# A transformer block on one core: one block of time-attention scores a step, layer-norm roots by ScalarE, and other forms of three VectorE operations

## The chip, the core and the metric

The kernel runs on one core of a Trainium2 chip. Five engines work side by side, each through its own instructions in order: TensorE (PE in the profile, its weight loads PEld), VectorE (DVE), ScalarE (ACT), GpSimd (POOL) and SyncE (SP), which here only issues DMA transfers. They wait for one another by semaphores. The metric is the device time of one execution, in microseconds (us). Lower is better.

## The reference, cut to what matters

The input `x` is (B, T, FB, C) = (2, 256, 128, 128) in float32. One layer has three parts, each with a layer norm ahead and a residual sum behind: causal attention along T (4 heads of 32), attention along FB with a band of 16 to each side (4 heads), and a feed-forward with a hidden width of 512.

```python
def _ln(x, w, b, eps=1e-05):
    mu = x.mean(-1, keepdims=True)
    var = ((x - mu) ** 2).mean(-1, keepdims=True)
    return (x - mu) * jax.lax.rsqrt(var + eps) * w + b

def _mha(x, wi, bi, wo, bo, h, mask):
    q, k, v = jnp.split(x @ wi.T + bi, 3, axis=-1)      # ... then split into h heads
    scores = jnp.einsum('...hqd,...hkd->...hqk', q, k) * (1.0 / np.sqrt(dh)) + mask
    attn = jax.nn.softmax(scores, axis=-1)
    o = jnp.einsum('...hqk,...hkd->...hqd', attn, v)
    return o.swapaxes(-2, -3).reshape(x.shape) @ wo.T + bo

xt = _ln(x, ln_t_w, ln_t_b).transpose(0, 2, 1, 3)
x = x + _mha(xt, t_wi, t_bi, t_wo, t_bo, H_T, causal).transpose(0, 2, 1, 3)
xf = _ln(x, ln_f_w, ln_f_b)
x = x + _mha(xf, f_wi, f_bi, f_wo, f_bo, H_F, band)
xn = _ln(x, ln_n_w, ln_n_b)
x = x + (jax.nn.gelu(xn @ w1.T + b1, approximate=False) @ w2.T + b2)
```

## The kernel before

The work is cut into groups of 4 tiles of 128 rows by 128 channels. All 128 `OverTime` groups (two sequences of 256 times in each) come first. Then runs of 8 `OverBands` groups and 8 `FeedForward` groups alternate, 16 runs in all. The software pipeline is a loop over steps `n`, and each step emits one stage of each of several groups: scores of group n, weighing of group n - 1, output of group n - 2, queries, keys and values of group n + 1, and so on down to loads of group n + 11. `InOrder` keeps each engine's instructions in the order in which they are emitted.

The layer norm of a group: statistics by VectorE, root by GpSimd, normalization by VectorE, then a turn to channel-major by a 32x32 transpose and a trip through DRAM.

```python
def root(self):
    self.rstd = path.small.tile([P, NT], F32, name="rstd", bufs=16)
    gpsimd.tensor_scalar(self.rstd, self.mv[:, :, 1], EPS, None, ALU.add)
    gpsimd.tensor_tensor(self.rstd, self.rstd, path.k.mhalf, ALU.pow)

def normalize(self):
    self.xh = path.work.tile([P, NT, P], F32, name="xh", bufs=2)
    for i in range(NT):
        vector.tensor_scalar(
            self.xh[:, i, :], self.src()[:, i, :], self.mv[:, i, 0:1], self.rstd[:, i : i + 1],
            ALU.subtract, ALU.mult,
        )
```

Scores lie as keys by queries. A head has 32 channels, so its scores use 32 rows of TensorE's array, and the four heads stand beside each other in four row tiles (`32*128` in the profile). All other attention products use column tiles (`128*32`) while an attention group is being weighed. In time attention a group has two sequences `s`, each of two key tiles: the first key tile meets 256 queries, the second 128. A step holds the block of `s = 0` at its start and that of `s = 1` after the weighing. Exponentials are by ScalarE, the causal mask by GpSimd, and the denominator takes a sum of two blocks, by GpSimd for `s = 0` and by VectorE for `s = 1`.

```python
class OverTime(Attention):
    W = 3 * P
    def scores(self, s):
        W, a = self.W, 2 * s * P
        self.sp = [path.bank([P, W], "sp") for h in range(H)]
        for h in range(H):
            r = rows_of(h)                                   # 32 rows of the head
            path.tensor.matmul(self.sp[h][:, 0 : 2 * P], self.kT[r, a : a + P], self.qT[r, a : a + 2 * P], ...)
        for h in range(H):
            r = rows_of(h)
            path.tensor.matmul(self.sp[h][:, 2 * P : W], self.kT[r, a + P : a + 2 * P], self.qT[r, a + P : a + 2 * P], ...)
    def weights(self, s):
        for h in range(H):
            path.scalar.activation(self.p[:, s, h, 0 : self.W], self.sp[h], AF.Exp)
    def mask(self, s):
        for n in (2, 0):
            gpsimd.affine_select(out=self.block(s, n), ...)          # 128 x 512
    def add(self, engine, s):
        engine.tensor_tensor(self.block(s, 3), self.block(s, 1), self.block(s, 2), ALU.add)
    # first_half: scores(0); second_half: scores(1); last_sum: add(vector, 1)
    # weigh: op of s = 0, rp (denominators, by a matrix of ones), op of s = 1
```

The division (`rp` and `op` lie in PSUM, the others in SBUF; `r0` is exp(-ln(rp)) by ScalarE, mended by one Newton step) and the band mask:

```python
# Attention.divide
vector.tensor_tensor(by_rows(t), by_tile(self.rp), by_tile(self.r0), ALU.mult)
vector.tensor_tensor(by_rows(u), by_tile(self.op), by_tile(self.r0), ALU.mult)
vector.scalar_tensor_tensor(self.oT, t, 2.0, u, ALU.subtract, ALU.mult)
# OverBands.second_mask, after the exponential; the other three heads are masked by GpSimd
for h in range(H - self.by_vector, H):                       # by_vector = 1
    blk = self.p[:, h]
    vector.tensor_tensor(blk, blk, path.band.unsqueeze(1).to_broadcast([P, NT, P]), ALU.mult)
```

The step, cut to its order:

```python
for n in range(-11, len(groups) + 2):
    do(n + 11, "load")
    do_at(n + 4, OverTime, "statistics")
    do(n, "first_half", "first_function", "first_mask")
    do_at(n + 2, Attention, "fetch")
    do_at(n + 3, Attention, "normalize", "turn")
    do_at(n + 4, OverTime, "root")
    do(n - 1, "weigh", "invert")
    do(n - 1, "divide")
    do(n, "second_half", "second_function", "second_mask", "bias")
    do_at(n + A, OverBands, "bias", "statistics", "root")    # A = 8 groups ahead
    do(n + 1, "queries_keys", "take_query", "take_key")
    do(n - 2, "output", "finish")
    do(n + 1, "values", "take_values")
    do(n, "last_sum")
    # ... cases of FeedForward and of the turns between kinds left out
```

Of the kernel before, what the change touches and what calls it, by code (L numbers as in the profile page):

```python
# [435 lines left out]
class Group:  # L436
# [32 lines left out]

    def normalize(self):  # L470
        path, vector = self.path, self.path.vector
        self.xh = path.work.tile([P, NT, P], F32, name="xh", bufs=2)
        for i in range(NT):
            vector.tensor_scalar(
                self.xh[:, i, :], self.src()[:, i, :], self.mv[:, i, 0:1], self.rstd[:, i : i + 1],
                ALU.subtract, ALU.mult,
            )
# [36 lines left out]
    def last_sum(self):  # L514
        pass

# [31 lines left out]
class Attention(Group):  # L548
    which = None

# [5 lines left out]
    def queries_keys(self):  # L556
        path = self.path
        wf = path.k.wf[self.which]
        self.qp = path.bank([P, NT * P], "qp")
        product(path, self.qp, wf[:, 0:P], self.xnT)  # L560

        self.kp = path.bank([P, NT * P], "kp")
        product(path, self.kp, wf[:, P : 2 * P], self.xnT)
# [11 lines left out]
    def values(self):  # L575
        path = self.path
        wv = path.k.wf[self.which][:, 2 * P : 3 * P]
        self.vp = path.bank([P, NT, P], "vp")
        for i in range(NT):
            product(path, self.vp[:, i], self.xnT[:, i * P : (i + 1) * P], wv)  # L580

    def take_values(self):
        path = self.path
        self.v = path.work.tile([P, NT, P], F32, name="v")
        path.scalar.copy(self.v, self.vp)
# [14 lines left out]
    def divide(self):  # L600

        path, vector = self.path, self.path.vector
        if self.r0 is None:
            self.oT = path.work.tile([P, NT * P], F32, name="oT", bufs=2)
            u = path.work.tile([P, NT * P], F32, name="u", bufs=2)
            vector.tensor_tensor(by_rows(u), by_tile(self.op), by_tile(self.r), ALU.mult)
            vector.tensor_scalar(self.oT, u, -1.0, None, ALU.mult)
            return
        t = path.work.tile([P, NT * P], F32, name="t", bufs=2)
        vector.tensor_tensor(by_rows(t), by_tile(self.rp), by_tile(self.r0), ALU.mult)  # L610
        u = path.work.tile([P, NT * P], F32, name="u", bufs=2)
        vector.tensor_tensor(by_rows(u), by_tile(self.op), by_tile(self.r0), ALU.mult)
        self.oT = path.work.tile([P, NT * P], F32, name="oT", bufs=2)
        vector.scalar_tensor_tensor(self.oT, t, 2.0, u, ALU.subtract, ALU.mult)

    def output(self):
        path = self.path
        self.yp = path.bank([P, NT, P], "yp")
# [22 lines left out]
class OverTime(Attention):  # L641

    which = 0
    W = 3 * P

    def scores(self, s):
        path = self.path  # L650
        W, a = self.W, 2 * s * P
        self.sp = [path.bank([P, W], "sp") for h in range(H)]
        for h in range(H):
            r = rows_of(h)
            path.tensor.matmul(
                self.sp[h][:, 0 : 2 * P], self.kT[r, a : a + P], self.qT[r, a : a + 2 * P], start=True, stop=True
            )
        for h in range(H):
            r = rows_of(h)
            path.tensor.matmul(  # L660
                self.sp[h][:, 2 * P : W], self.kT[r, a + P : a + 2 * P], self.qT[r, a + P : a + 2 * P],
                start=True, stop=True,
            )

    def weights(self, s):
        path = self.path
        for h in range(H):
            path.scalar.activation(self.p[:, s, h, 0 : self.W], self.sp[h], AF.Exp)

    def mask(self, s):  # L670
        path = self.path
        for n in (2, 0):
            blk = self.block(s, n)
            path.gpsimd.affine_select(
                out=blk, in_=blk, compare_op=ALU.is_ge, fill=path.zero, base=0,
                pattern=[[0, H], [1, P]], channel_multiplier=-1,
            )

    def block(self, s, n):
        return self.p[:, s, :, n * P : (n + 1) * P]  # L680

    def add(self, engine, s):
        engine.tensor_tensor(self.block(s, 3), self.block(s, 1), self.block(s, 2), ALU.add)

    def first_half(self):
        self.p = self.path.work.tile([P, 2, H, self.W + P], F32, name="pt", tag="p", bufs=2)
        self.scores(0)

    def first_function(self):
        self.weights(0)  # L690

    def first_mask(self):
        self.mask(0)
        self.add(self.path.gpsimd, 0)

    def second_half(self):
        self.scores(1)

    def second_function(self):
        self.weights(1)  # L700

    def second_mask(self):
        self.mask(1)

    def last_sum(self):
        self.add(self.path.vector, 1)

    def weigh_one(self, op, s):
        path, p, v, W = self.path, self.p, self.v, self.W
        for h in range(H):  # L710
            r = rows_of(h)
            path.tensor.matmul(op[r, s, :], v[:, 2 * s, r], p[:, s, h, 0 : 2 * P], start=True, stop=False)
        for h in range(H):
            r = rows_of(h)
            path.tensor.matmul(
                op[r, s, P : 2 * P], v[:, 2 * s + 1, r], p[:, s, h, 2 * P : W], start=False, stop=True
            )

    def weigh(self):
        path = self.path  # L720
        op = path.bank([P, 2, 2 * P], "op")
        rp = path.bank([P, 2, 2 * P], "rp")
        self.weigh_one(op, 0)
        sums = self.p.rearrange("p s h (n q) -> p s h n q", q=P)[:, :, :, 0:4:3, :]
        for h in range(H):
            path.tensor.matmul(rp[rows_of(h), :, :], path.k.ones[:, 0:D], sums[:, :, h], start=True, stop=True)
        self.weigh_one(op, 1)
        self.op = op.rearrange("p s q -> p (s q)")
        self.rp = rp.rearrange("p s q -> p (s q)")


class OverBands(Attention):
# [14 lines left out]
    def first_function(self):  # L747
        for h in range(H):
            self.path.scalar.activation(self.p[:, h].rearrange("p i q -> p (i q)"), self.sp[h], AF.Exp)
# [11 lines left out]
    def second_mask(self):  # L761
        path = self.path
        for h in range(H - self.by_vector, H):
            blk = self.p[:, h]
            path.vector.tensor_tensor(blk, blk, path.band.unsqueeze(1).to_broadcast([P, NT, P]), ALU.mult)

    def first_half(self):
        self.p = self.path.work.tile([P, H, NT, P], F32, name="pf", tag="p", bufs=2)
        self.scores(range(H))

    def weigh(self):
        path = self.path
        self.rp = path.bank([P, NT * P], "rp")
        for h in range(H):
# [3 lines left out]
            )  # L778
        self.op = path.bank([P, NT * P], "op")
# [7 lines left out]
class FeedForward(Group):  # L787
# [21 lines left out]
    def first_half(self):  # L809
        self.hp = {}  # L810
        self.hT = self.path.work.tile([P, self.path.k.NI, NT * P], F32, name="hT")
# [41 lines left out]
class BoundedPath:  # L853
    def __init__(self, ctx, tc, k):
# [4 lines left out]
        self.ps = ctx.enter_context(tc.tile_pool(name="ps", bufs=8, space=PSUM))  # L859
# [4 lines left out]
        once = ctx.enter_context(tc.tile_pool(name="once", bufs=1))  # L864

        self.band = once.tile([P, P], F32, name="band")
        tc.nc.gpsimd.memset(self.band, 1.0)
        for s in (1, -1):
            tc.nc.gpsimd.affine_select(
                out=self.band, in_=self.band, compare_op=ALU.is_ge, fill=0.0, base=BAND,  # L870
# [3 lines left out]
    def bank(self, shape, name):  # L874
        return self.ps.tile(shape, F32, name=name, tag="ps")
# [12 lines left out]
    def quad(self, held, name, bufs):  # L888

        held[name] = self.xpool.tile([P, NT, NT, P], F32, name=name, tag=name, bufs=bufs)  # L890

    def groups(self, x, out):
# [3 lines left out]
        for b in range(B):  # L896
            for f0 in range(0, FB, GA):
# [17 lines left out]
                def part(name, g, held=held):  # L915
                    if name == "res" and name not in held:
                        self.quad(held, "res", 2)
                    return held[name][:, :, g]
# [3 lines left out]
        for b in range(B):  # L922
            for r0 in range(0, T, RUN):
                run = []
                for t0 in range(r0, r0 + RUN, GB):
# [20 lines left out]
                    def part(name, g, held=held):  # L946
                        if name == "res" and name not in held:
                            self.quad(held, "res", 2)
                        return held[name][:, g]
# [7 lines left out]
    def run(self, x, out):  # L957
# [17 lines left out]
        for n in range(-11, len(groups) + 2):  # L975
            feeds = [at(n - 2 + i, FeedForward) for i in range(5)]
            bands = [at(n - 2 + i, OverBands) for i in range(5)]
            turn = feeds[2] and bands[1]
            self.by_columns = at(n - 1, Attention)
            do(n + 11, "load")  # L980
            do_at(n + 4, OverTime, "statistics")
# [3 lines left out]
            do(n, "first_half", "first_function", "first_mask")  # L985
            if turn:
                do(n, "second_half", "second_function")
            do_at(n + 2, Attention, "fetch")
            do_at(n + 1, FeedForward, "fetch")
            do_at(n + 2, FeedForward, "normalize", "turn")  # L990
            do_at(n + 3, Attention, "normalize", "turn")
            do_at(n + 4, OverTime, "root")
            if bands[2]:
                do(n, "second_mask")
            do(n - 1, "weigh")
            do(n - 1, "invert_exactly" if turn else "invert")
            if bands[2] or turn:
                do(n - 2, "output", "finish")
            do(n - 1, "divide")
            do_at(n + 5, FeedForward, "statistics")  # L1000
            if not turn:
                do(n, "second_half", "second_function")
            if not bands[2]:
                do(n, "second_mask", "bias")
# [3 lines left out]
                if not turn:  # L1008
                    do_at(n + A, OverBands, "statistics", "root")
            do(n + 1, "queries_keys", "take_query", "take_key")  # L1010
            if not bands[2] and not turn:
                do(n - 2, "output", "finish")
            do(n + 1, "values", "take_values")
            do(n, "last_sum")
# [69 lines left out]
```

## Time and profile before

| what | value |
|---|---|
| time, median of 3 runs | 2785.62 us (2785.54 to 2787.24) |
| profiled span | 2785.2 us |
| granted TensorE clock | 0.999 |
| instructions | 103938 |

The profile has one row for each instruction. A float32 product of TensorE stands in it as two matmul instructions. "Busy" is the union of an engine's instructions, and the ends of matmuls are modelled, so that a busy PE does not have to be a PE at its best. Groups are named `out<-in` by the program's tiles: `sp` scores, `pt` and `pf` weights of time and band attention, `op` weighed values, `rp` denominators, `yp` output product, `qp`, `kp`, `vp` query, key and value products, `hp` and `zp` the two feed-forward products, `xh` the normalized rows, `z` and `turned` their turn. Almost all rows carry line L848, that of the helper `InOrder`, so one goes by tiles.

### The profile page before, as it was taken

To read this page: it belongs to the slowest core of one execution; us is meant where nothing else is said; L and a number is where in the kernel's file an instruction comes from. 1 tells how busy PE (TensorE), PEld (TensorE's weight loads), DVE (VectorE), ACT (ScalarE), POOL (GpSimd) and SP (SyncE) were. 2 spreads that over 40 slices of the span, in tenths; PEclk is the share of its full clock that TensorE was granted. 3 is DMA by queue.
4 is the path that set the end of the run, shared out by engine and by line. 5 is a ranking of instruction groups with operands and counts; after the bars stand their busy time and mean duration, and the time that the engine had idled before them with its cause. 6 is when DMAs were issued, how large, how long until landed. Compare 5 with 4: busy or idle time off the path is not lost.

```text
span 2785.2 us, 103938 instructions
## 1 busy us (share of the span) xinstructions
PE 2730.3 (98%) x42534; PEld 1867.5 (67%) x42534; DVE 2221.5 (80%) x6446; ACT 1800.0 (65%) x3328; POOL 2079.3 (75%) x2569
## 2 busy tenths in 40 slices
PE   4999999999999989999999999999999999999998
PEld 3666666666666657776777777777777767767776
DVE  5888888888888898778678687687786786876874
ACT  2888888878888866646556556456466465574563
POOL 3899999999999997667676676676676666766762
PEclk9999999999999999999999999999999999999999
DMA  5555555555555554544544544535545445444333
GB/s 121 135 147 137 137 141 143 146 132 146 139 142 135 146 134 117 129 117 102 140 105 111 132 106 123 130 100 127 127 99 137 104 108 130 113 117 114 91 92 85
DMA packets 471301, 343.70 MB, mean 123 GB/s; under 512 B 43296, under 2 KB 405152, under 8 KB 470816
## 3 DMA queue, kind: packets, MB, share of 16 engines
q1 hardware_dynamic: 469568, 335.92, 47.5%
q8 instruction: 337, 5.52, 0.9%
q14 instruction: 148, 1.21, 0.2%
q10 hardware_dynamic: 1248, 1.05, 0.1%
HBM read 169.03 MB, written 167.77 MB: 121 GB/s over the span
## 4 chain that ended last, share of the span: by engine, by line
PE 93%; DVE 3%; DMA 2%; POOL 1%; issue 0%; SPq 0%; ACT 0%; DVEq 0%; POOLq 0%
PE zp L848 17%; PE hp L848 16%; PE sp L848 12%; PE op L848 10%; PE qp L848 8%; PE rp L848 8%; PE vp L848 8%; PE yp L848 7%; PE kp L848 7%; POOL pt L848 1%; DMA x<-in_x 1%; DVE xh L848 1%; DMA xnT<-turned 1%; DVE oT L848 0%; POOL rstd L848 0%; DVE stats L848 0%
## 5 line engine op out<-in xcount | busy, mean ns | idle before, releaser
L848 ACT ACTIVATE hT<-hp,b 128x512 f32<-128x512 f32 x512 | 348.7, 687 | 546.0 <-PE hp L848 536.1
L848 POOL TENSOR_SCALAR_AFFINE_SELECT pf<-pf 128x512 f32<-128x512 f32 x768 | 541.5, 720 | 173.5 <-ACT pf L848 147.1
L848 PEld LDWEIGHTS zp<-w2T_sb,hT 128*128 128x128 f32 x4096 | 476.4, 192 | 56.1 <-issue 54.0
L848 DVE TENSOR_SCALAR xh<-x,mv,rstd 128x128 f32<-128x128 f32 x1536 | 509.2, 392 | 0.4 <-POOL rstd L848 0.4
L848 PE MATMUL zp<-w2T_sb,hT 128*128 128x128 f32 x4096 | 479.8, 275 | 0.1
L848 PE MATMUL hp<-xnT,w1f 128*128 128x512 f32 x1024 | 469.2, 596 | 3.6 <-DMA xnT<-turned 3.4
L848 POOL TENSOR_TENSOR rstd<-rstd,mhalf 128x4 f32<-128x4 f32 x384 | 441.3, 1149 | 32.0
L848 ACT ACTIVATE pt<-sp 128x384 f32<-128x384 f32 x1024 | 419.5, 497 | 58.8 <-PE sp L848 58.8
L848 PE MATMUL sp<-qT,kT 32*128 32x128 f32 (+1 forms) x8192 | 389.5, 315 | 0.8 <-ACT kT L848 0.8
L848 POOL TENSOR_SCALAR_AFFINE_SELECT pt<-pt 128x512 f32<-128x512 f32 x512 | 322.7, 651 | 79.0 <-ACT pt L848 79.0
L848 PEld LDWEIGHTS sp<-qT,kT 32*128 32x128 f32 x8192 | 310.9, 185 | 79.7 <-issue 31.1
L848 POOL TENSOR_SCALAR rstd<-mv 128x4 f32<-128x4 f32 x384 | 89.2, 232 | 365.5 <-DVE mv L848 365.1
L848 DVE BATCH_NORM_STATS2 stats<-x 128x6 f32<-128x128 f32 x1536 | 329.0, 274 | 7.6 <-DMA x<-in_x 7.6
L848 ACT ACTIVATE pf<-sp 128x512 f32<-128x512 f32 x512 | 264.3, 603 | 58.8 <-PE sp L848 52.4
L848 PEld LDWEIGHTS hp<-xnT,w1f 128*128 128x128 f32 x1024 | 182.2, 190 | 178.9 <-issue 109.6
L848 PE MATMUL qp<-xnT,wf 128*32 128x512 f32 (+1 forms) x1856 | 273.1, 600 | 26.2 <-DVE xh L848 26.2
L848 PEld LDWEIGHTS yp<-wn,oT 128*32 128x32 f32 (+1 forms) x7808 | 240.8, 111 | 84.0 <-issue 63.2
L848 PEld LDWEIGHTS vp<-wf,xnT 128*32 128x32 f32 (+1 forms) x7424 | 241.1, 113 | 70.4 <-issue 60.2
L848 DVE STREAM_TRANSPOSE z<-xh 128x512 f32<-128x512 f32 x384 | 273.2, 711 | 18.9 <-DMA turned<-z 5.8
L848 PE MATMUL yp<-wn,oT 128*32 128x128 f32 (+1 forms) x7808 | 277.9, 273 | 0.3 <-DVE t L848 0.3
L848 DVE TENSOR_TENSOR res<-zp,res 128x512 f32<-128x512 f32 x128 | 87.6, 685 | 234.8 <-PE zp L848 234.7
L848 PE MATMUL vp<-wf,xnT 128*32 128x128 f32 (+1 forms) x7424 | 273.5, 273 | 0.5 <-DVE t L848 0.5
(90 smaller groups left out, 4072.8 us busy)
## 6 DMA issues: line engine op xcount, KB each, us to landing
turned<-z SPq DMA_DIRECT2D x1536, 64.0 KB, 2.2
xnT<-turned SPq DMA_DIRECT2D x384, 256.0 KB, 2.8
x<-in_x SPq DMA_DIRECT2D x128, 256.0 KB, 4.8
x<-res SPq DMA_DIRECT2D x256, 128.0 KB, 3.4
x<-x SPq DMA_DIRECT2D x128, 256.0 KB, 4.1
out<-res SPq DMA_DIRECT2D x256, 128.0 KB, 2.4
w1T_sb<-in_w1T ACTq DMA_DIRECT2D x1, 256.0 KB, 3.9
w2T_sb<-in_w2T ACTq DMA_DIRECT2D x1, 256.0 KB, 4.2
```

The lines of the kernel that those rows point to most:

```text
L848: return self.tc.keep_in_program_order(emit(*args, **kwargs))
```

## The change

Six parts belong together.

1. **One block of scores a step.** A step now holds, for time attention, the second key tiles of group n and the first key tiles of group n + 1, for both sequences, in one block of 16 products in an order that mixes 128- and 256-column products over the four row tiles. The 8 PSUM banks are given out by name for it and turned over from step to step. Queries, keys and values move one step ahead (group n + 2). Exponentials become 128x512 for first tiles and 128x256 for second tiles, and a mask call covers both sequences.
2. **Sums.** Both sums of the denominator go to GpSimd; VectorE's `last_sum` goes.
3. **Roots by ScalarE.** For time groups (and the first band groups) GpSimd's add and power become Ln and Exp of ScalarE, with one Newton step of three small VectorE operations.
4. **`xh`.** Its four operations take 129 elements in 3 runs of 43, with the destination's rows spaced 130 apart, [...].
5. **Division.** The Newton step is done in place in PSUM, and the last product takes `op` from PSUM, so that no operation has two inputs in SBUF.
6. **Band mask.** VectorE adds 0 or -1e30 to the scores of one head in PSUM ahead of the exponential, instead of multiplying the weights in SBUF behind it.

The diff, cut to its core:

```diff
+    def root_by_scalar(self):
+        path.scalar.activation(ln, self.mv[:, :, 1], AF.Ln, bias=path.eps)
+        path.scalar.activation(self.root0, ln, AF.Exp, scale=-0.5)
+    def refine(self):
+        vector.scalar_tensor_tensor(t, self.mv[:, :, 1], EPS, y, ALU.add, ALU.mult)
+        vector.scalar_tensor_tensor(t, t, -0.5, y, ALU.mult, ALU.mult)
+        vector.scalar_tensor_tensor(self.rstd, t, 1.5, y, ALU.add, ALU.mult)
 ...
     def normalize(self):
+        run, odd = P + 2, P + 1
+        xh = path.work.tile([P, NT * run], F32, name="xh", bufs=2)
+        self.xh = xh.rearrange("p (t w) -> p t w", w=run)[:, :, 0:P]
         for i in range(NT):
+            a = 1 if i == NT - 1 else 0
             vector.tensor_scalar(
-                self.xh[:, i, :], self.src()[:, i, :], self.mv[:, i, 0:1], self.rstd[:, i : i + 1],
-                ALU.subtract, ALU.mult,
+                xh[:, i * run - a : i * run - a + odd].rearrange("p (r w) -> p r w", r=3), self.src(i, a),
+                self.mv[:, i, 0:1], self.rstd[:, i : i + 1], ALU.subtract, ALU.mult,
             )
 ...
-        vector.tensor_tensor(by_rows(t), by_tile(self.rp), by_tile(self.r0), ALU.mult)
+        vector.tensor_tensor(self.rp, self.rp, self.r0, ALU.mult)
-        vector.tensor_tensor(by_rows(u), by_tile(self.op), by_tile(self.r0), ALU.mult)
+        vector.scalar_tensor_tensor(u, self.rp, 2.0, self.r0, ALU.subtract, ALU.mult)
-        vector.scalar_tensor_tensor(self.oT, t, 2.0, u, ALU.subtract, ALU.mult)
+        vector.tensor_tensor(by_rows(self.oT), by_tile(self.op), by_tile(u), ALU.mult)
 ...
+def time_scores(old, new):
+    for h, second, s in (
+        (0, 1, 0), (1, 0, 0), (2, 0, 0), (3, 1, 0), (0, 1, 1), (3, 1, 1), (0, 0, 0), (3, 0, 0),
+        (1, 0, 1), (2, 0, 1), (0, 0, 1), (3, 0, 1), (1, 1, 0), (2, 1, 0), (1, 1, 1), (2, 1, 1),
+    ):
+        if second and old is not None:
+            old.second_scores(h, s)      # 128 columns into bank b<h>
+        if not second and new is not None:
+            new.first_scores(h, s)       # 256 columns into bank a<h>
 ...
     def first_function(self):            # OverBands
+        for h in range(H - self.by_vector, H):
+            sp = self.sp[h].rearrange("p (i q) -> p i q", i=NT)
+            path.vector.tensor_tensor(sp, sp, path.band.unsqueeze(1).to_broadcast([P, NT, P]), ALU.add)
         for h in range(H):
-            self.path.scalar.activation(self.p[:, h].rearrange("p i q -> p (i q)"), self.sp[h], AF.Exp)
+            path.scalar.activation(self.p[:, h].rearrange("p i q -> p (i q)"), self.sp[h], AF.Exp)
 ...                                     # the step of the loop
+            old, new = (groups[i] if at(i, OverTime) else None for i in (n, n + 1))
+            if old is not None or new is not None:
+                time_scores(old, new)
+                b = self.banks
+                Attention.place = dict(rp=b["b0"], op=b["b3"], yp=b["a1"], qp=b["a2"], kp=b["b1"], vp=b["b2"])
+            if old is not None:
+                old.second_weights(old.late)         # heads 0, 3
+            if new is not None:
+                new.first_weights(new.early)         # heads 1, 2
+            if old is not None:
+                old.second_weights(old.early)
+                old.mask_second()
+                old.add(0)
+            do_at(n + 5, OverTime, "statistics")
+            do_at(n + 4, OverTime, "normalize", "turn")
             do(n - 1, "weigh")
             do(n - 1, "invert_exactly" if turn else "invert")
+            if new is not None:
+                new.first_weights(new.late)
+                new.mask_first()
+            if old is not None:
+                old.add(1)
+            if bands[2] or turn or old is not None:
                 do(n - 2, "output", "finish")
             do(n - 1, "divide")
+            do_at(n + 2, OverTime, "queries_keys", "take_query", "take_key")
+            do_at(n + 5, OverTime, "root_by_scalar", "refine")
+            if at(n - 1, OverTime):
+                do_at(n + A - 1, OverBands, "root_by_scalar", "refine")
+            do_at(n + 2, OverTime, "values", "take_values")
```

## The prediction

> **What bounds the kernel now.** I began with the page's busy shares and its slices, to see which engine has no room.
>
> ```profile
> PE 2730.3 (98%) x42534; PEld 1867.5 (67%) x42534; DVE 2221.5 (80%) x6446; ACT 1800.0 (65%) x3328; POOL 2079.3 (75%) x2569
> PE   4999999999999989999999999999999999999998
> ```
>
> TensorE is without a gap but for the fill in the first slice and one slice near 1000 us. So an operation that another engine loses is worth nothing by itself, and the question is what the change does to TensorE. Busy time doesn't tell whether the matmuls run at their best, so I next took the chain of waits inside the time-attention stage, over one whole step (start, length, product, instructions):
>
> ```profile
> 302.25 1.00 PE qp L848 x8
> 303.24 0.86 PE kp L848 x8
> 304.10 0.87 PE yp L848 x32
> 304.97 0.87 PE vp L848 x32
> 305.85 0.86 PE sp L848 x16
> 306.71 0.79 PE op L848 x16
> 307.50 0.86 PE rp L848 x8
> 308.36 0.65 PE op L848 x16
> 309.01 0.86 PE sp L848 x16
> 309.87 0.99 PE qp L848 x8
> ```
>
> The chain stays on PE, and the step is 309.87 - 302.25 = 7.62 us (two later starts of qp, 500.47 and 508.10, say 7.63). The measure of full speed is in the view itself: kp, rp, yp and vp stream 512 columns (rp, kp in one product a head or tile, vp and yp in four of 128) in 0.86 to 0.87, which is 1.68 ns a column. A block of scores is 256 + 128 = 384 columns a row tile, the tiles side by side, and should take 0.645; it takes 0.86, **0.215 too much**. The product that follows a block pays too: qp 1.00 where kp is 0.86 (0.135), and the first op 0.79 where the second, of the same shape, is 0.65 (0.14). Together a block of scores costs about 0.355 us beyond its columns, twice a step. Nothing else in the step is off by more than 0.02.
>
> Then the stage's sums (us, then busy time and instructions of PE, PEld, DVE, ACT, POOL; clock; DMA), for steady time attention, its last steps, and bands with feed-forward:
>
> ```profile
> 300.00:600.00 300.00, 300.00 (x5972) 188.93 (x5968) 264.49 (x712) 241.76 (x513) 276.31 (x316) 1.00 0.53 138
> 960.00:1036.00 76.00, 68.41 (x1380) 43.18 (x1376) 73.92 (x184) 53.70 (x113) 74.68 (x84) 1.00 0.49 125
> 1100.00:1500.00 400.00, 399.18 (x5193) 284.92 (x5196) 301.15 (x919) 231.34 (x380) 267.79 (x349) 1.00 0.48 121
> ```
>
> 300 us are 39.3 steps of 7.63: DVE 6.73, ACT 6.15 and POOL 7.03 us a step. POOL is next behind PE with 0.6 us of room. In the last eight steps of the stage, 965.69 to 1036.13 by the starts of qp (70.4 us), PE has gaps and POOL is busy for 98%: there it is the bound, because those steps carry the bias and root of the first bands as well. From 1100 us on PE is full again.
>
> [...] only the row-tiled sp among column-tiled products costs extra, 0.355 us a visit. [...] The groups of the same 300 us agree:
>
> ```profile
> L848 POOL TENSOR_TENSOR res<-x,orow 128x512 f32<-128x512 f32 x40 | 68.6, 1716 | 0.0
> L848 POOL TENSOR_TENSOR pt<-pt 128x512 f32<-128x512 f32 x40 | 51.5, 1287 | 0.0
> L848 POOL TENSOR_TENSOR rstd<-rstd,mhalf 128x4 f32<-128x4 f32 x39 | 54.7, 1401 | 3.2
> L848 DVE TENSOR_SCALAR xh<-x,mv,rstd 128x128 f32<-128x128 f32 x160 | 57.5, 418 | 0.0
> L848 DVE TENSOR_TENSOR pt<-pt 128x512 f32<-128x512 f32 x39 | 40.6, 1041 | 2.7 <-POOL pt L848 1.1
> L848 DVE BATCH_NORM_STATS2 stats<-x 128x6 f32<-128x128 f32 x157 | 33.8, 273 | 0.0
> ```
>
> POOL's bias, which lies beside VectorE's two-input sum of pt, takes 1716 ns where its sum of the same size takes 1287; xh, 128 elements, takes more than the statistics of 128 elements. [...]
>
> **Part by part.**
>
> *Scores.* The columns stay: 2 x 256 + 2 x 128 = 768 a row tile. One visit in place of two removes one cost of 0.355, about 0.36 us a step. That asks that the four tiles stream independently although their products differ in length. The trace supports it: near 1509.9 us products of yp in two column tiles start before the last of op in the other two, so the tiles don't march in one line. [...] New step: 7.63 - 0.36 = **7.27 us**.
>
> *Whether the others keep up with 7.27.* POOL: masks 99.1 / 39.3 = 2.52 (the same elements in half as many calls), two sums of 1.287 = 2.57, bias 1.29 to 1.72; the roots (1.40 + 0.23) go. Together 6.4 to 6.8. DVE: 6.73, less its sum 40.6 / 39.3 = 1.03, xh from 57.5 / 39.3 = 1.46 to some 0.87 (four at the 33.8 / 157 = 0.215 of the statistics), more three small operations at the 0.15 of the aggregation: about 5.6. ACT: exponentials cover the same columns, plus two of 4 elements; [...] All three fit[...].
>
> *Order within the step.* From the first score at 0: scores to 1.53[...], rp to 2.4, op 3.7, yp 4.5, qp 5.4, kp 6.3, vp 7.15. ACT, taking v of the step before until about 0.8, has its second-tile and first early exponentials done by 3.0, Ln and Exp of rp (ready at 2.6) by 4.2, the late exponentials by 5.3, waits for qp, and ends kT at 7.1 to 7.2, just when the next scores need it. That is the tightest joint. POOL begins the masks at 3.0 and ends the second sum at 8.1, 0.8 into the next step, where rp's second half wants it at 1.96. DVE gets yp at 4.7 and ends oT at 7.5, wanted 3.4 us later. Each bank is free before its next writer.
>
> *Sum.* The first 120 of the 128 time steps: 120 x 0.36 = 43.2 us. In the last eight POOL falls to 6.6 + 1.29 for the bands' bias = 7.9: 8 x 7.9 = 63.2 in place of 70.4, 7.2 us. One more stage ahead of the weighing lengthens the fill by about half a step; I take off 3. Bands and feed-forward: PE has 399.18 of 400 us and its products are untouched, so lighter xh, division and mask give 0. Together 43.2 + 7.2 - 3 = 47 us: 2785.6 - 47 = **2738 us** (-1.7%).
>
> **The rivals.** (a) *A new wait takes the gain*: kT late for the scores, or ACT not closing in 7.27. For it: [...] its chain ends within 0.1 us of need. Against it: in the bands kp, vp and scores follow in this same order, and by the view of waits the matmuls of sp waited for kT 0.8 us in all and their weight loads 20.2 us in 98 places, 0.2 each[...]. If the step became 7.45, the gain would be 120 x 0.18 + 6 - 3 = 25, and the time 2761. (b) *Tiles of unequal length don't overlap*: with products started in line, the mixed order leaves tiles empty, some 0.3 us a step, and almost nothing remains but the stage's end: about 2780. Against it is the trace near 1509.9. (c) [...] for it are the 0.8 us that PE lacks in 400; against it is the same number. It could give 2 to 4 us over the stage, at the turns. (d) *The end of the stage and the fill do better than I think*: were the last eight steps also at 7.27, 58.2 in place of 63.2, the time would be 2733; without the 3 us of fill, 2730.
>
> **Range and chances.** The low end takes (c) and (d) together, 2726; the high end a step of 7.43 or so, 2758. Over 2% faster means below 2729.9, so it needs every small thing at once: 0.2. A loss of more than 2% would need steps of over 8.1 us, with no engine near that: 0.04.
>
> **What would show it right or wrong.** Right: the distance from qp to qp in the steady stage falls from 7.63 to 7.25 to 7.30, with sp in one piece of about 1.5 us and rp behind it 0.13 longer than kp; op has no long piece; POOL's bias falls towards 1290 ns and the mean of xh towards 270; between 1100 us and the end nothing moves. Wrong by rival (a): PE's sp waits for ACT kT, or ACT shows no idle time. Wrong by (b): the block of scores takes well over 1.6 us with PE waiting for nothing. Wrong in the sum: bands and feed-forward steps (6.44 and 7.01 us between starts of qp and of zp) change.

## The result, and the profile after

| | median us | ratio to before (95% interval) |
|---|---|---|
| before | 2786.43 | |
| after | 2971.16 | 1.0663 (1.0645 to 1.0681) |

The changed kernel is **slower by 6.6%**, 184.7 us, where 47 us of gain were predicted. The page's busy shares and slices, of after:

```profile
PE 2811.1 (95%) x43522; PEld 1959.0 (66%) x43522; DVE 2458.9 (83%) x6727; ACT 1860.0 (63%) x3600; POOL 1870.9 (63%) x2169
PE   5999999999999989999999999999999999999998
PE 70%; DVE 22%; DMA 4%; issue 3%; SPq 1%; ACT 0%; DVEq 0%; POOL 0%
```

and the last of these three of before:

```profile
PE 93%; DVE 3%; DMA 2%; POOL 1%; issue 0%; SPq 0%; ACT 0%; DVEq 0%; POOLq 0%
```

By the first two lines little has changed: PE still looks full in almost every slice. Only the third, the shares of the chain that ended last, says that DVE holds 22% of it, where it held 3%. The modelled ends of PE's matmuls hide waits, so the loss has to be looked for in the distances between starts. I read these off the records of qp and zp and, for the whole, off three marks: the first product hp (the end of time attention and of the first eight groups of bands), the distance between the starts of two runs of feed-forward (15 periods, each of eight groups of bands and eight of feed-forward), and the end.

| | before | after | difference |
|---|---|---|---|
| a step of steady time attention, us | 7.63 | 7.81 | +0.18 |
| first hp | 1082.3 | 1136.4 | +54.1 |
| mean period | 108.91 | 117.39 | +8.48, x 15 = +127 |
| last run of hp to the end | 69.2 | 72.2 | +3 |

So both stages lose. By the starts of rp, 41.6 of the 54.1 us ahead of the first hp are lost in the first 120 steps (120 times 0.18 are 22 of them, the others lie in the fill and in single steps of 9.3 and 10.9 us), 4.5 in the last eight, and 8.0 in the first eight groups of bands. So three quarters of the loss (8 + 127 + 3) lie where nothing was expected. The granted TensorE clock may have a part in it as well: 0.988 in after, 0.999 before, and 0.93 from 1000 to 1100 us, where PE is busy for 90.88 us. As an estimate from the two means, its part is at most 0.011 x 2970 = 33 us. In e1 and e5 below the clock is 0.998 again; what brings it down was not tested. The sums by stretch, of after (us, busy time and instructions of PE, PEld, DVE, ACT, POOL; clock; DMA share; GB/s):

```profile
900.00:1000.00 100.00, 100.00 (x2060) 69.83 (x2056) 97.81 (x260) 84.78 (x194) 75.87 (x65) 1.00 0.58 139
1100.00:1500.00 400.00, 374.84 (x5113) 259.77 (x5107) 312.69 (x868) 218.80 (x361) 238.68 (x333) 0.99 0.44 106
```

In time attention DVE is busy for 97.81 of 100 us: it has become the bound. In bands and feed-forward PE has lost 25 of 400 us, though DVE is idle for more than a fifth of the time.

**Time attention.** The chain of waits inside it (start, length, product, instructions), of after, over one step of DVE:

```profile
by line: DVE xh L871 47.3%; DVE stats L871 9.8%; issue 9.0%; DVE u L871 8.8%; DVE oT L871 8.7%; DVE res L871 8.1%; DVE rp L871 7.8%; DVE vy L871 3.3%; DVE mv L871 2.5%; DVE rstd L871 2.0%; DVE z L871 0.4%
982.48 2.98 DVE xh L871 x4
985.45 0.02 issue
985.48 0.04 DVE z L871
985.51 0.60 issue
986.11 0.65 DVE res L871
986.76 0.62 DVE rp L871
...
987.41 0.70 DVE u L871
...
988.13 0.69 DVE oT L871
988.83 0.10 DVE vy L871
...
989.31 0.78 DVE stats L871 x4
990.09 0.20 DVE mv L871 x3
990.29 2.98 DVE xh L871 x4
```

The chain never leaves DVE, from one xh to the next: 990.29 - 982.48 = 7.81. The four operations of xh, 129 elements each, take 2.98 us of it, more than res, rp, u and oT together (2.66), which have 512 each. What lies beside them is in the timeline, of after:

```profile
943.37 2.98 DVE L871 TENSOR_SCALAR xh<-x,mv,rstd 128x129 f32<-128x129 f32 x4
943.78 1.12 POOL L871 TENSOR_SCALAR_AFFINE_SELECT p<-p 128x1024 f32<-128x1024 f32 x1 [1.80 <-ACT p L871]
...
944.98 1.28 POOL L871 TENSOR_TENSOR p<-p,p 128x512 f32<-128x512 f32 x1
...
946.39 0.71 DVE L871 STREAM_TRANSPOSE z<-xh 128x512 f32<-128x512 f32 x1
```

xh starts, POOL begins its mask 0.4 us later, then its sum, and xh ends within 0.1 us of that sum's end (946.26). The tile view (shortest, median and longest, ns) of after gives 313/348/1460 from 300 to 900 us: alone the operation takes a third of a microsecond, beside POOL as long as POOL's instructions. The third of these four starts at 943.86, beside the mask (943.78 to 944.90), and ends at 944.98; the fourth lasts from 944.90 to 946.35, until the sum is over. It is so everywhere: 715 of the 1536 operations of xh in after take over 500 ns, and each of these ends at most 92 ns behind the end of a POOL instruction. So an xh that meets POOL's work stands until POOL's instruction is over; it is called blocked from here on. Part 4 of the change was meant to let xh run beside POOL. That a form of 3 runs of 43 would do so was the author's estimate, and no trace of before shows it. Nor was it tried here, by the record of the operands in after: both source and destination stand there as one run of 129 elements, not as 3 runs of 43. The runs are adjacent in memory, and they were merged on the way to the instruction. So the form of part 4 was not in the kernel that ran.

**Bands.** DVE's timeline over one step of bands, of after:

```profile
1226.69 0.70 DVE L871 TENSOR_TENSOR sp<-sp,band 128x512 f32<-128x512 f32 x1 [0.62 <-PE sp L871]
1227.30 2.63 DVE L871 TENSOR_SCALAR xh<-x,mv,rstd 128x129 f32<-128x129 f32 x4
1229.96 0.71 DVE L871 STREAM_TRANSPOSE z<-xh 128x512 f32<-128x512 f32 x1
1230.60 0.83 DVE L871 BATCH_NORM_STATS2 stats<-x 128x6 f32<-128x128 f32 x4
1231.35 0.36 DVE L871 BATCH_NORM_AGGREGATE mv<-stats 128x2 f32<-128x6 f32 x4
1231.62 0.66 DVE L871 TENSOR_TENSOR x<-yp,x 128x512 f32<-128x512 f32 x1
1232.20 0.69 DVE L871 TENSOR_TENSOR rp<-rp,r 128x512 f32<-128x512 f32 x1
1232.92 0.69 DVE L871 SCALAR_TENSOR_TENSOR u<-rp,r 128x512 f32<-128x512 f32 x1
1233.65 0.69 DVE L871 TENSOR_TENSOR oT<-op,u 128x512 f32<-128x512 f32 x1
1234.96 0.70 DVE L871 TENSOR_TENSOR sp<-sp,band 128x512 f32<-128x512 f32 x1 [0.62 <-PE sp L871]
```

and PE's beside it:

```profile
1231.91 0.49 PE L871 MATMUL sp<-qT,kT 32*128 32x128 f32 x4
1233.76 1.16 PE L871 MATMUL sp<-qT,kT 32*128 32x128 f32 x28 [1.36 <-DVE u L871]
```

The two engines wait for each other in a ring. DVE's step opens with the band mask, which now needs PE's last scores (sp of the fourth head). Behind it DVE, which works in order, does xh, z, the statistics of a feed-forward group and then rp and u. PE's next scores have 4 of their 32 instructions done, the beginning of two heads, and then stand, because the third head's bank is one that u frees. Only after u come the other scores, and only after those the next band mask. One turn is 1234.96 - 1226.69 = 8.27 us where PE's products need 6.44. The view of waits has this one, "PE sp <- DVE u", with 89.1 us in 90 places. Two things in this step do not stand among the six parts of the change: the diff also moves the statistics of feed-forward groups from behind the division to a place ahead of it, and in the bands it holds a bank back for yp.

From the first to the last qp of a run of bands a period loses 5.75 of its 8.48 us (50.99 against 45.24 in the mean of 15 runs). The other 2.7 lie between there and the next run's start, on the way through the feed-forward groups, and were not traced by themselves.

### The profile page after: what moved, and what is told of

It reads as the page before. It is cut to its first block, busy times and chain, and to the rows that moved or that the text cites. A ratio compares the mean times of both kernels' runs of the same rounds, so it can differ in the third digit from the quotient of the medians.

```text
span 2969.6 us, 105850 instructions
## 1 busy us (share of the span) xinstructions
PE 2811.1 (95%) x43522; PEld 1959.0 (66%) x43522; DVE 2458.9 (83%) x6727; ACT 1860.0 (63%) x3600; POOL 1870.9 (63%) x2169
## 4 chain that ended last, share of the span: by engine, by line
PE 70%; DVE 22%; DMA 4%; issue 3%; SPq 1%; ACT 0%; DVEq 0%; POOL 0%
PE hp L871 15%; PE zp L871 14%; PE sp L871 11%; DVE xh L871 10%; PE op L871 6%; PE rp L871 5%; PE yp L871 5%; PE vp L871 4%; PE qp L871 4%; PE kp L871 4%; DVE u L871 3%; DVE rp L871 2%; DVE stats L871 2%; DVE z L871 2%; DMA xnT<-turned 1%
## 5 line engine op out<-in xcount | busy, mean ns | idle before, releaser
L871 DVE TENSOR_SCALAR xh<-x,mv,rstd 128x129 f32<-128x129 f32 x1536 | 861.7, 623 | 0.0
L871 POOL TENSOR_SCALAR_AFFINE_SELECT pf<-pf 128x512 f32<-128x512 f32 x768 | 478.1, 637 | 363.1 <-ACT pf L871 336.9
L871 PE MATMUL sp<-qT,kT 32*128 32x128 f32 (+1 forms) x8192 | 460.5, 320 | 100.7 <-DVE u L871 89.1
L871 PEld LDWEIGHTS sp<-qT,kT 32*128 32x128 f32 x8192 | 375.0, 186 | 184.6 <-issue 86.6
L871 POOL TENSOR_SCALAR_AFFINE_SELECT p<-p 128x1024 f32<-128x1024 f32 x256 | 286.5, 1119 | 271.2 <-ACT p L871 271.1
L871 ACT ACTIVATE p<-sp 128x512 f32<-128x512 f32 (+1 forms) x1024 | 422.5, 491 | 37.7 <-PE sp L871 24.3
L871 POOL TENSOR_TENSOR p<-p,p 128x512 f32<-128x512 f32 x256 | 329.8, 1288 | 10.7
L871 ACT ACTIVATE qT<-qp,bq 128x512 f32<-128x512 f32 x256 | 176.0, 687 | 195.5 <-PE qp L871 195.5
L871 PE MATMUL qp<-xnT,wf 128*32 128x512 f32 (+1 forms) x1850 | 267.1, 593 | 28.3 <-DMA xnT<-turned 26.3
L871 POOL TENSOR_SCALAR rstd<-mv 128x4 f32<-128x4 f32 x248 | 56.5, 228 | 372.8 <-DVE mv L871 372.8
```

Source lines behind the costliest of these rows:

```text
L871: return self.tc.keep_in_program_order(emit(*args, **kwargs))
```

## The experiments

The theory after this reading has two parts. **P**: xh, which reaches VectorE as one run of 129, is blocked wherever POOL works beside it, and would not be in a form whose runs stay apart. **R**: the ring in the bands, made of the band mask ahead of the exponential, the statistics ahead of the division, and a long xh. The rivals: the extra element and the spacing of 130 cost the time themselves; the new division or the held bank cost it. Four kernels have one edit in the changed kernel, five combine such edits, and one edits the kernel before.

### e1: xh in runs that stay apart

Five runs of 32 elements a tile, each followed by a gap of one (160 elements, of which 128 are used; the first or last run is taken from the neighbouring tile), so that the runs of the destination don't touch. The source is one run of 160.

```diff
-        xh = path.work.tile([P, NT * run], F32, name="xh", bufs=2)
+        xh = path.work.tile([P, 5 * NT * (D + 1)], F32, name="xh", bufs=2)
+        runs = xh.rearrange("p (r w) -> p r w", w=D + 1)
-                xh[:, i * run - a : i * run - a + odd].rearrange("p (r w) -> p r w", r=3), self.src(i, a),
+                runs[:, 5 * i - a : 5 * i - a + 5, 0:D], self.src(i, a),
```

> Theory P [...]: in the changed kernel the three runs of 43 lie end to end, so that source and destination of xh stand in the records as one run of 129 each, [...] and xh waits for whole GpSimd instructions. Here the destination is 5 runs of 32 with a gap between them and the source one run of 160. If P holds, xh falls from 561 ns each to about 260 to 300 and never over 400, time attention runs at 7.29 us a step in place of 7.81 (some 60 us), the bands' steps lose 1 to 1.5 us each as well, and the time is 2810 to 2860. [...] Theory O (order of VectorE's work in the bands) expects time attention to gain as said, and the bands' steps to stay over 7 us.

Measured: **2798.50 us**, ratio 1.0051 (1.0034 to 1.0068), below the expected range. The first hp is at 1047.3, steps in time attention take 7.29 to 7.40, a period 111.97. The same moment of a step, of e1:

```profile
609.40 1.09 POOL L871 TENSOR_SCALAR_AFFINE_SELECT p<-p 128x1024 f32<-128x1024 f32 x1 [1.30 <-ACT p L871]
609.50 1.58 DVE L871 TENSOR_SCALAR xh<-x,mv,rstd 128x160 f32<-128x160 f32 x4
...
610.58 1.29 POOL L871 TENSOR_TENSOR p<-p,p 128x512 f32<-128x512 f32 x1
...
611.11 0.71 DVE L871 STREAM_TRANSPOSE z<-xh 128x512 f32<-128x512 f32 x1
```

xh now runs through POOL's mask and into its sum without a stop. Its longest instance from 300 to 900 us is 443 ns:

```profile
L871 DVE TENSOR_SCALAR xh<-x,mv,rstd x328: 402/431/443, 302.1 to 896.1; 128x160 f32<-128x160 f32 x164
```

Over the whole run the mean of the 1536 operations is 430 ns, and in e5 below, which has the same form, none of those from 1200 to 1600 us takes more than 442 ns. The expected 260 to 300 ns were too low for 160 elements. P is shown: this one edit takes away 172.7 of the 184.7 us, and in time attention PE is busy for 300.00 of 300 us again, at 7.32 a step. A period keeps 3 us too many; the two steps of 8.27 take 7.32 and 7.25.

### e2: xh as it was, in the new step

```diff
-                xh[:, i * run - a : i * run - a + odd].rearrange("p (r w) -> p r w", r=3), self.src(i, a),
+                xh[:, i * run : i * run + P], self.src(i, a),
```

> xh with 128 elements as before the change, all else as in the changed kernel. Theory P [...] expects no change: xh 550 to 570 ns each, 2955 to 2980 us. A rival by which the 129 form itself is slow (odd length, a start that is off by one) expects xh at the 331 ns of before and the time attention at 7.3 to 7.6 us a step, 2900 or less.

Measured: 2960.58 us, 1.0642 (1.0624 to 1.0659); first hp 1125.4, period 117.39, steps of 7.81. The tile view from 300 to 900 us, of e2:

```profile
L871 DVE TENSOR_SCALAR xh<-x,mv,rstd x306: 309/1108/1461, 299.2 to 894.9; 128x128 f32<-128x128 f32 x153
```

and the same instruction in the kernel before:

```profile
L848 DVE TENSOR_SCALAR xh<-x,mv,rstd x316: 304/334/816, 300.4 to 895.8; 128x128 f32<-128x128 f32 x158
```

The extra element is not the cause: without it the kernel is only 10.6 us quicker. The spacing of 130 stays in e2, but its quickest xh takes 309 ns against 304 before, so nothing shows that the spacing costs. One and the same operation of 128 elements has a median of 334 ns in the step of before and of 1108 in the new one. VectorE's own order around it is the same in both, statistics ahead and turn behind; what the change did to xh was to bring it together in time with POOL's masks and sums: over the whole run 197 of the 1536 operations take over 500 ns in before, and 715 in after.

### e3 and e4: the two other members of the ring

e3 puts the band mask back behind the exponential, as a product in SBUF; xh and all else as in the changed kernel.

```diff
-        for h in range(H - self.by_vector, H):                     # first_function
-            path.vector.tensor_tensor(sp, sp, path.band..., ALU.add)
+    def second_mask(self):                                         # ahead of weigh
+        for h in range(H - self.by_vector, H):
+            path.vector.tensor_tensor(blk, blk, path.band..., ALU.mult)
```

> The band mask of the fourth head again as a multiplication behind the exponential, behind xh and turn in VectorE's order. Theory O (the addition at the head of VectorE's step ties all of VectorE's step to TensorE's last score, and the bank that the next scores need is freed at the end of it) expects the bands' steps to fall from 7.24 and 8.27 to 6.5 to 7.0 and the turn from 17.7 towards 15.5, 16 runs of some 6 us, so 2860 to 2900; time attention stays at 7.81. Theory P expects a small change, since xh is blocked all the same: 2940 to 2980.

e4 only moves the statistics of feed-forward groups behind the division.

```diff
-            do_at(n + 5, FeedForward, "statistics")
 ...
             do(n - 1, "divide")
+            do_at(n + 5, FeedForward, "statistics")
```

> The statistics of the feed-forward groups behind the division in VectorE's order, as before the change. Theory O: they lie in the loop from the band addition over division to the next scores, and the steps that have them are 1.03 us longer (8.27 against 7.24), so those steps fall to about 7.24 and the bands gain 16 x 2 to 4 us: 2905 to 2940. If they lie in the shade of a wait, no change: 2960 to 2980.

Measured: e3 2883.26 us, 1.0352 (1.0335 to 1.0369), period 112.64; e4 2872.35 us, 1.0313 (1.0296 to 1.0331), period 111.64. The step in time attention stays at 7.81 in both, as it must. In e4 the two steps of 8.27 come down to 7.24 and 6.51. DVE in the second of these, of e4:

```profile
1215.83 0.69 DVE L871 TENSOR_TENSOR rp<-rp,r 128x512 f32<-128x512 f32 x1
1216.56 0.69 DVE L871 SCALAR_TENSOR_TENSOR u<-rp,r 128x512 f32<-128x512 f32 x1
1217.28 0.69 DVE L871 TENSOR_TENSOR oT<-op,u 128x512 f32<-128x512 f32 x1
1217.89 0.86 DVE L871 BATCH_NORM_STATS2 stats<-x 128x6 f32<-128x128 f32 x4
1218.67 0.37 DVE L871 BATCH_NORM_AGGREGATE mv<-stats 128x2 f32<-128x6 f32 x4
1218.99 0.70 DVE L871 TENSOR_TENSOR sp<-sp,band 128x512 f32<-128x512 f32 x1
```

The statistics now lie where DVE used to wait for PE's scores, and the 8.27 - 7.24 = 1.03 us by which the first of the two falls are their 1.02 us in the ring of after (1231.62 - 1230.60 there). In the second xh is not blocked any more either: its four operations take 1.11 us, where they took 2.63. So R is shown too: mending any one of its three members gives back 4.8 to 5.8 of the 8.5 us a period (e3 4.8, e1 5.4, and e4 5.8, which was more than expected). Their sum, 15.9, is nearly twice the loss, so the gains overlap: with one member mended a step can gain little more before it reaches the 6.44 us that PE needs.

### e5, e6, e7: the parts together

e5 is e1 with e4; e6 is that with e3 as well; e7 is e5 without the bank that the bands hold back for `yp`.

```diff
-        path.held_bank = path.turn_of_bank()      # e7 alone
```

> The changed kernel with xh in five separated runs [...] and the feed-forward statistics behind the division. Time attention 7.31 us a step as in the first experiment, some 38 us less than before the change. In the bands VectorE's loop from the band addition to the next scores loses 1.03 us of statistics and 1.3 of blocked xh and comes to about 6 us, under the 6.44 that TensorE needs, so the period of a run (8 band and 8 feed-forward groups) falls from 113.6 to 108.7 to 110. Theory: two faults explain the loss, and the sum is 2740 to 2770, below the kernel before. If a third part (band addition, held bank) costs by itself, the period stays over 111 and the time near 2790.

> As the one before, with the band mask behind the exponential again. If the band addition costs nothing [...], this is the same within 8 us (2740 to 2770), or slower[...]; if the addition at the head of VectorE's step is a fault of its own, this is 10 to 40 us faster than the one before.

> As the first of these, with the banks of the bands in plain turn (yp's bank taken when yp is written). The third head's scores then take the bank of rp and the fourth those of op, which is now read last, after u: VectorE's loop gets one operation (0.72 us) longer. If that loop is under TensorE's 6.44 us anyway, no change (within 5 us); if it is the bound, 16 runs of up to 8 x 0.7: up to 60 us more.

| | median us | ratio (95% interval) | first hp | period |
|---|---|---|---|---|
| e5 | 2763.18 | 0.9918 (0.9904 to 0.9931) | 1044.4 | 110.01 |
| e6 | 2771.91 | 0.9954 (0.9940 to 0.9967) | 1044.7 | 110.34 |
| e7 | 2790.89 | 1.0017 (1.0010 to 1.0024) | 1047.1 | 111.46 |

With both causes mended the change is **faster than the kernel before**, by 0.8%. The place of the band mask is worth nothing any more (e6 is even 8.7 us behind e5). The held bank is good: without it the steps of bands in the middle of a run take 6.90 instead of 6.44 to 6.51, and the whole 27.7 us more. So the held bank is not what costs. The new division was not undone alone in any run.

### e9: the new xh alone, in the kernel before

xh in e1's form in the kernel before, with two buffers for `hT` as in the changed one (three before), and nothing else.

```diff
-        self.xh = path.work.tile([P, NT, P], F32, name="xh", bufs=2)
+        xh = path.work.tile([P, 5 * NT * (D + 1)], F32, name="xh", bufs=2)
...
-        self.hT = self.path.work.tile([P, self.path.k.NI, NT * P], F32, name="hT")
+        self.hT = self.path.work.tile([P, self.path.k.NI, NT * P], F32, name="hT", bufs=2)
```

> The kernel before the change, with xh alone in five separated runs [...] (and two buffers in place of three for the hidden layer, as in the change, for room). There TensorE sets the step and VectorE's xh is beside it: xh at 330 to 440 ns each and never over 450, time within 5 us of before (2780 to 2790), a gain if any in the eight steps at the end of time attention. [...]

Measured: 2799.81 us, 1.0051 (1.0037 to 1.0065): **slower** by 0.5%, where no change was expected. The first hp does not move (1082.5 against 1082.3), since PE was the bound there. A period grows by 0.9 us; the longer xh (428 ns in the mean from 1100 to 1500 us, where it had 375) or the buffer of hT may be the reason, and this run doesn't part them. An xh that POOL doesn't block has no value of its own in the kernel before; in the changed one it makes room for the new order of scores and shortens the ring.

### e10 and e11: where the new form is needed

e10 is e5 with the new form for time attention alone; elsewhere xh takes 128 elements as before. e11 gives the bands back everything they had: that xh, the band mask behind the exponential, the old division, the banks in their plain turn; the statistics stay behind the division.

```diff
+        if not isinstance(self, OverTime):                          # normalize: e10 and e11
+            for i in range(NT):
+                vector.tensor_scalar(xh[:, i * P : (i + 1) * P], self.src()[:, i, :], ...)
+            return
...
+        if not isinstance(self, OverTime):                          # divide: e11
+            vector.tensor_tensor(by_rows(t), by_tile(self.rp), by_tile(self.r0), ALU.mult)
+            vector.tensor_tensor(by_rows(u), by_tile(self.op), by_tile(self.r0), ALU.mult)
+            vector.scalar_tensor_tensor(self.oT, t, 2.0, u, ALU.subtract, ALU.mult)
+            return
```

> [...] in bands and feed-forward in its old form of 128 elements; feed-forward statistics behind the division; band addition and new division everywhere. Time attention as in the runs before with five runs: first hp at 1044 to 1048 us. For the period of a run two theories part: if what still costs there is the longer xh of 160 elements, the period falls from 110.0 to 109.0 and the time to about 2750; [...] the period goes back to about 111.6, that of the run with the statistics behind alone, and the time to about 2785.

> As the one beside it, with the bands wholly as before the change: band mask behind the exponential, old division, banks in plain turn. The time attention's gain (first hp at 1044 to 1048 in place of 1082) with the old period of 108.9: 1046 + 15 x 108.9 + 69 = 2749, so 2745 to 2755. If the period stays over 110, something else that the change moved in the bands (buffers of the hidden layer, order of loads) costs.

Measured: e10 2806.28 us, 1.0071 (1.0057 to 1.0084), first hp 1058.0, period 111.71. e11 **2756.11 us, 0.9901 (0.9886 to 0.9916)**, first hp 1050.5, period 108.93. The stretches of e11, its xh in the second of them, and DVE over one step of bands:

```profile
300.00:600.00 300.00, 300.00 (x6564) 209.21 (x6560) 291.40 (x820) 263.75 (x616) 242.09 (x205) 1.00 0.57 146
1200.00:1600.00 400.00, 400.00 (x5515) 280.10 (x5518) 305.28 (x921) 241.11 (x398) 270.26 (x356) 1.00 0.46 118
...
L889 DVE TENSOR_SCALAR xh<-x,mv,rstd x232: 305/338/1305, 1202.1 to 1599.8; 128x128 f32<-128x128 f32 x116
...
1232.70 1.11 DVE L889 TENSOR_SCALAR xh<-x,mv,rstd 128x128 f32<-128x128 f32 x4
1233.85 0.71 DVE L889 STREAM_TRANSPOSE z<-xh 128x512 f32<-128x512 f32 x1
1234.97 1.17 DVE L889 TENSOR_TENSOR pf<-pf,band 128x512 f32<-128x512 f32 x1 [0.41 <-ACT pf L889]
1236.07 0.68 DVE L889 TENSOR_TENSOR x<-yp,x 128x512 f32<-128x512 f32 x1
1236.67 0.67 DVE L889 TENSOR_TENSOR t<-rp,r 128x512 f32<-128x512 f32 x1
1237.26 0.67 DVE L889 TENSOR_TENSOR u<-op,r 128x512 f32<-128x512 f32 x1
```

e10 was a miss of both expectations for the time. The second, that an xh which POOL can block costs in the bands as well, had its period: such an xh in the bands costs 1.7 us a period and 14 us ahead of the first hp as long as the bands keep the rest of the ring. In e11 xh is still blocked at times (its longest took 1305 ns), but it and its turn lie ahead of the mask, where DVE waits anyhow. Between that wait and the end of u DVE has the mask, x, t and u, 2.96 us (1234.97 to 1237.93), where after has 6.92 (1226.69 to 1233.61). The period is that of before to 0.02 us, and PE shows no gap in the second stretch.

Where time attention turns into bands, a blocked xh still costs in e11: from 989.71 on its four operations take 4.03 us beside POOL's sums and biases, PE's scores wait 3.04 us for the oT behind them, and the first hp comes 6.1 us later than in e5. So in these runs a blocked xh does harm where PE waits for what lies behind it, and none was seen elsewhere.

e11 undoes several parts at once; which of them takes the last 1.1 us a period between e5 and e11 off was not tried apart. It is the best version found, 30 us below before.

## Why the prediction was wrong, point by point

Two steps of it failed: that the new xh runs beside POOL unhindered, and that bands and feed-forward give 0. Either alone is enough to miss: with the first mended the time is 2798.5 us (e1), with the second mended in part 2872.4 (e4), with both 2763.2 (e5). The gain of time attention was rightly reasoned: 38 of the 47 us are there in e5.

- **PE bounds the kernel; a visit of row-tiled scores costs 0.355 us; one visit less makes the step 7.27.** Right. Where DVE gets out of the way, steps take 7.29 to 7.40, 7.32 in the mean (e1, e5, e11), with few longer ones. In e1 rp starts 1.56 us after the first score (1.53 were predicted, well over 1.6 was the mark of rival (b)), so tiles of unequal length do stream side by side, and rival (b) falls. Of (a) little is left: the weight loads of sp wait 0.2 us for kT in every step of e1 (44.4 us in the whole run), which may be part of the 0.05 us over 7.27.
- **xh at "some 0.87" us a step.** This is the first step that failed. The 0.87 took for granted that the new form is not blocked by POOL. That was the author's estimate, made for the pattern as written (3 runs of 43) and not for the one that reaches the engine (one run of 129 in source and destination). Instead of the predicted 0.87 us a step, the four operations took 2.98. In e1's form the blocking is gone (443 ns at most from 300 to 900 us, where after has 1460); what in the form does it is not shown.
- **DVE "about 5.6" of 7.27.** Wrong by more than that one error. In the changed kernel it is 97.81 of 100 us, 7.64 a step. But even in e1 it is 291.39 / 300 x 7.31 = 7.1: e1's xh is 63.3 us for 41 steps, 1.54 a step instead of 0.87, and the refinement has a term that I put at 0.15 and that takes 1.06 (below). The new step fits with 0.2 us to spare, not with 1.7.
- **POOL's bias at 1716 ns beside VectorE's sum, where POOL's own sum takes 1287.** Rightly read as the two engines holding each other up, and underrated: I counted only what an xh that is never blocked would bring, not what a blocked one would cost once it met POOL's work. e2 against before, 1108 against 334 ns, is that cost.
- **POOL 6.4 to 6.8, and ACT fits in 7.27.** Right or on the safe side: in e11's steady stage POOL has 242.09 and ACT 263.75 of 300 us, 5.9 and 6.4 a step. The bias fell from 1716 ns to 1275 in after, where VectorE's sum is gone, as expected. The small roots of ACT, 4 elements each, take 300 and 206 ns.
- **The division without two SBUF inputs.** Worth nothing in time attention: rp, u and oT take 689 to 692 ns each there (e1), and the old three had 659, 675 and 693 in the same stage of before.
- **"Bands and feed-forward: ... give 0."** This is the second step that failed, by some 138 us (8 ahead of the first hp, 127 in the 15 periods, 3 at the end). That PE had 399.18 of 400 us said only that nothing *was* waiting. The diff also moved two operations of DVE across PE's joints: the mask ahead of the exponential, the statistics ahead of the division. I read them as lighter, and didn't draw the ring that they close with u and its bank. The prediction named a change of these steps as a sign of its error, but gave it no number and no share of the 4% for a loss. Rival (c), a gain of 2 to 4 us there, falls with it.
- **47 us for time attention.** With xh mended it is 1082.3 - 1044.4 = 38 in e5, so the mechanism was right and a size was off by a fifth. By the starts of rp in e5 the fill costs 3.7 us where 3 were predicted, the first 120 steps gain 37.4 for 43.2, and the last eight 4.7 for 7.2. The term that was mis-sized most is thus the gain of a step, 0.31 us for 0.36.

## What to carry to other kernels

A form of access that is to change how an operation runs must be looked up in the record of the instruction, not in the source; adjacent runs may arrive as one, as three of 43 stand as one of 129 in after. An engine that runs without a gap doesn't protect a stage: when an operation of another engine moves across the place where that engine takes or gives a bank, draw the ring of waits and add up its length before putting the stage down as 0. And an operation that another engine can block should lie away from that engine's long work, or outside every ring; in e11's runs of bands, with no ring over it, an xh of up to 1305 ns cost nothing (a period of 108.93 us, 108.91 in before).

## What the hardware showed that was not expected

An operation of 4 elements can cost a microsecond. The first operation of the refinement, of e1 from 300 to 900 us, and the one right behind it:

```profile
L871 DVE SCALAR_TENSOR_TENSOR vy<-mv,root x83: 903/1049/1185, 299.7 to 899.8; 128x4 f32<-128x4 f32 x83
L871 DVE SCALAR_TENSOR_TENSOR vy<-vy,root x82: 161/163/166, 300.8 to 893.6; 128x4 f32<-128x4 f32 x82
```

The first comes while POOL works and stands until POOL's instruction has ended: in e1 one starts at 599.71, 0.2 us after POOL's bias, and ends at 600.79, 0.02 us after it. The longest in the changed kernel, 1227 ns from 594.24, likewise ends 0.02 us after POOL's bias (594.18 to 595.44). The second comes when that instruction is over, and its longest in e1 is 166 ns. In the changed kernel, where xh has waited already, the median of the first is 164 ns, so part of the wait that e1 takes from xh has only moved here. In e1 and e11 this one operation takes over 1 us of a step of 7.3.

Also, a POOL mask over 1024 elements took 1121 ns in time attention of after, where one over 512 took 648 in that of before: a merged call is cheaper than two. And xh as one run of 128 or 129 elements takes 304 to 313 ns at its best, while 160 elements in e1's form take 431: the first saves some 0.12 us, and being blocked once by POOL (up to 1460 ns for one operation) costs more than that.
